# A fused RWKV and mixture-of-experts block: a reordered front, row differences on GpSimd, products of zeros at the start, one table for the slots' tokens

## The chip, the cores and the metric

The kernel runs on one core of a Trainium2 chip. The metric is the device time of one execution in microseconds. Three runs of the kernel before gave 666.15, 668.23 and 668.59 us, so the median is 668.23 us. Engines are named as in the profile: PE is the matrix engine, PEld its weight loads, DVE the vector engine, ACT the scalar engine, POOL is GpSimd, and SP issues most of the DMAs.

## The reference, cut to what matters

The input x has 2 x 2048 tokens of 256 channels. All weights are float32.

```
xn = layernorm(x)
# attention part (RWKV): a second layernorm with ln_g, ln_b
xa = layernorm(xn) * ln_g + ln_b
last = xa of the token before (zero for the first token of a sequence)
k, v, r = (xa*mix + last*(1-mix)) @ W.T          # one mix and one W for each of k, v, r
num, den = scans over the tokens: den = den*td + exp(k); num = num*td + exp(k)*v
attn = (sigmoid(r) * num/(den + 1e-8)) @ Wo.T
# expert part: 8 experts, the best 2 of each token
scores = relu(xn @ Wr + br);  weights = softmax over the best two
ffn = sum over the two: weight * (relu(xn @ W1[e] + b1[e]) @ W2[e] + b2[e])
out = x + attn + ffn
```

## The kernel before

The 4096 tokens are worked on in 8 blocks of 512 tokens (four groups of 128 partitions). The kernel has two parts. **The front** normalises, transposes and scores all blocks, chooses two experts for each token, sorts the 8192 (token, expert) pairs into slots of 128 rows that share one expert, and computes k, v and r. **The expert part** then walks over the slots: it gathers the slot's rows from a table in HBM, multiplies by W1 and W2 of the slot's expert (lines 818 and 831) and scatters the result with an add; the scans of the attention part (lines 697 to 729) run in between on DVE.

The order of the front is written out by hand: the schedule is manual, so every engine executes its instructions in the order of the program text, and each engine's queue is strictly in order. The pieces of the front, with the lines of the profile:

- `stats(b)` (187 to 196): DVE takes mean and variance of the block's four groups (8 instructions); POOL makes from them the factor `rr` by a power (193, 195) and a second value (196).
- `normed(b)` (214 to 222): DVE makes `mrr` from `rr`, then DVE normalises three groups (219) and ACT one (221); SP writes the rows to the table.
- `turned(b)` (232 to 240): POOL sets or copies the first column of `xaT` (the token before the block), PE transposes the rows (8 products, 238), ACT evacuates each half of the channels twice: `x2T` for the scores (239) and `xaT` for the attention (240).
- `scored(b)` and `routed(b)` (251 to 262): 8 small products for the scores, an evacuation by ACT, a transpose.
- `mix(n)`: the next n blends. A block has three (k, v, r). Ahead of a block's first one DVE makes the difference of neighbouring tokens `dx` (271, one buffer, 1024 elements a partition); a blend is two instructions on DVE (275).
- `some(n)`: the next n of 48 projection pieces, six for each block. A piece is two logical products (301, four records in the profile) and one evacuation by ACT (304). Blend number i, counted from 0, feeds pieces 2i and 2i+1.
- `divisors` (202): a power of 16 columns on POOL; `undivided` and `best_two` (206 to 353): the choice of experts on DVE, after all blocks are scored.
- then counts, ranks and positions of the pairs (484 to 576, mostly small DVE instructions), and the sorting into slots: eight rounds in which DVE builds tables `oh_a`, `oh_b` (645) and `oh_t` (656), and PE multiplies (665) for each of 8 columns `oh_a` by `oh_b` and by `oh_t` into the two halves of `inv`: the first half counts whether a slot's place is taken, the second holds its token number less 2048. DVE makes from both the rows to gather and to write (672 to 680); `experts_of_places` (590 to 632) finds the expert of each slot, `whose_i`.

The loads of the first slots' weights start once `whose_i` exists (the SP queue reads it into a register); the gathers start once `frm` (680) exists. Blends and pieces of the later blocks are spread among the steps after the choice of experts, so that PE has work beside them.

Of the kernel before, what the change touches and what calls it, by code (L numbers as in the profile page):

```python
# [9 lines left out]
F32 = mybir.dt.float32  # L10
# [16 lines left out]
def rwkv_moe_block(  # L27
# [21 lines left out]
    nc = tc.nc  # L49
# [130 lines left out]
    def stats(b):  # L180
        def mk(nm, shape):
            return rpool.tile(shape, F32, bufs=1, name=f"{nm}_{b}")

        st = mk("st", [P, NS, 6])
        mv = mk("mv", [P, NS, 2])
        for i in range(NS):
            nc.vector.bn_stats(st[:, i, :], xts[b][:, i, :])
            nc.vector.bn_aggr(mv[:, i, :], st[:, i, :])
        mean, var = mv[:, :, 0], mv[:, :, 1]

        at = ts(b, NS)
        w = mk("w", [P, NS])
# [4 lines left out]
        mrrs[b] = (mean, mk("mrr", [P, NS]))  # L197

    def divisors(half):

# [10 lines left out]
    def normed(b):  # L211
        xt = xts[b]
        mean, mrr = mrrs[b]
        nc.vector.scalar_tensor_tensor(mrr, mean, -1.0, rrs[b], ALU.mult, ALU.mult)
        x2 = x2s[b] = rpool.tile([P, NS, C], F32, tag="x2", bufs=3, name=f"x2_{b}")
        for t in range(NS):
            r, m = rrs[b][:, t : t + 1], mrr[:, t : t + 1]
            if t:
                nc.vector.tensor_scalar(x2[:, t, :], xt[:, t, :], r, m, ALU.mult, ALU.add)
            else:  # L220
                nc.scalar.activation(x2[:, t, :], xt[:, t, :], AF.Identity, bias=m, scale=r)
        nc.sync.dma_start(table_t[:, ts(b, NS), 0:C], x2)
# [3 lines left out]
    def turned(b):  # L226
        x2 = x2s[b]
        x2T = x2Ts[b] = rpool.tile([P, NC, TB], F32, tag="x2T", name=f"x2T_{b}")

        xaT = xaTs[b] = xa_pool.tile([P, NC, TB + 1], F32, name=f"xaT_{b}")  # L230
        if b % BPS == 0:
            nc.gpsimd.memset(xaT[:, :, 0:1], 0.0)
        else:
            nc.gpsimd.tensor_copy(xaT[:, :, 0:1], xaTs[b - 1][:, :, TB : TB + 1])
        for c in range(NC):
            tp = ps_t.tile([P, TB], F32, tag="pt", name=f"tp_{b}_{c}")
            for t in range(NS):
                nc.tensor.transpose(tp[:, ts(t, P)], x2[:, t, ts(c, P)], ident)
# [20 lines left out]
    def routed(b):  # L259
        i = b * NS % HT  # L260
        sp = sps[b * NS // HT][:, i : i + NS, :]
        nc.tensor.transpose(sp.rearrange("p t e -> p (t e)"), s8s[b], ident)

    blends = [[] for _ in range(NB)]

    def blender():
        for b in range(NB):
            now, last = xaTs[b][:, :, 1 : TB + 1], xaTs[b][:, :, 0:TB]

            dx = mixes.tile([P, NC, TB], F32, tag="dx", bufs=1, name=f"dx_{b}")  # L270
            nc.vector.tensor_tensor(dx, now, last, ALU.subtract)
            for i in range(3):
                m = mixes.tile([P, NC, TB], F32, tag="mix", name=f"mix{i}_{b}")
                for c in range(NC):
                    nc.vector.scalar_tensor_tensor(  # L275
                        m[:, c, :], dx[:, c, :], vec(1 + i, c), last[:, c, :],
                        ALU.mult, ALU.add,
                    )
                blends[b].append(m)
                yield  # L280
# [3 lines left out]
    def mix(n):  # L284
        for _ in range(n):
            next(blending)
# [115 lines left out]
    token = count("token", NT, F16, base=-NTOK // 2, step=P, chan=1)  # L402

    rest_row = rout.tile([P, NU], F32, name="rest_row")
    nc.gpsimd.iota(
# [9 lines left out]
    zero = rpool.tile([P, C], F32, bufs=1, name="zero")  # L415
    nc.gpsimd.memset(zero, 0.0)

    stats(2)
    normed(1)
    scored(0)  # L420
    turned(1)
    nc.scalar.activation(td, cols[:, E * NH : E * NH + NC], AF.Exp)
    mix(3)
    routed(0)
    scored(1)
    normed(2)
    some(2)
    turned(2)
    routed(1)
    stats(3)  # L430
    stats(4)
    normed(3)
    some(2)
    scored(2)
    turned(3)
    divisors(0)
    routed(2)
    mix(3)
    some(2)
    scored(3)  # L440
    routed(3)
    stats(5)
    normed(4)
    some(2)
    turned(4)
    stats(6)
    normed(5)
    some(1)
    scored(4)
    turned(5)  # L450
    stats(7)
    normed(6)
    routed(4)
    some(1)
    scored(5)
    turned(6)
    divisors(1)
    normed(7)
    routed(5)
    some(1)  # L460
    scored(6)
    turned(7)
    mix(3)
    routed(6)
    some(1)
    scored(7)
    routed(7)
    undivided()
    best_two()
    nc.sync.dma_start(  # L470
        b1cols.rearrange("e p h -> p e h"),
# [7 lines left out]
    some(4)  # L479


    pre = ps_t.tile([P, 2, E * NT], F32, tag="pt", name="pre")
# [10 lines left out]
    mix(3)  # L493
    some(2)
    cum = rt("cum", (P, E, NT))
    cum_flat = cum.rearrange("p e t -> p (e t)")
# [51 lines left out]
    nc.vector.tensor_tensor(pos, pos, be(delta), ALU.mult)  # L548
    nc.vector.tensor_tensor(pos, pos, rank, ALU.add)
    nc.vector.tensor_tensor(pos, pos, be(base_f), ALU.add)  # L550
    some(6)
    mix(3)
    some(6)
    mix(1)

    g2 = rt("g2", (P, NT))
    nc.gpsimd.tensor_tensor(g2, e2, g1, ALU.mult)
# [20 lines left out]
    mix(2)  # L578
    some(2)


# [53 lines left out]
        )  # L635


    inv = ps_y.tile([P, 2 * NU], F32, tag="py", name="inv")
    opool = routing.enter_context(tc.tile_pool(name="opool", bufs=3))
    for i0 in range(0, K * NT, CH):  # L640
# [21 lines left out]
        mix((0, 0, 0, 1, 0, 1, 0, 2)[i0 // CH])  # L662
        for i in range(CH):
            for j, right in enumerate((bq, bt_)):
                nc.tensor.matmul(
                    inv[:, j * NU : (j + 1) * NU], a[:, i // 2, :, i % 2],
                    right[:, i // 2, :, i % 2],
                    start=(i0 + i == 0 and j == 0), stop=(i0 + i == K * NT - 1 and j == 1),
                )
        some((1, 1, 1, 1, 1, 2, 1, 0)[i0 // CH])  # L670
    invs = rt("invs", (P, 2, NU))
    nc.vector.tensor_copy(invs, inv.rearrange("p (a u) -> p a u", a=2))
# [9 lines left out]
    experts_of_places()  # L682
    routing.close()
    gpool = ctx.enter_context(tc.tile_pool(name="gpool", bufs=3, side="right"))
    wpool = ctx.enter_context(tc.tile_pool(name="wpool", bufs=2, side="right"))
# [161 lines left out]
    load_first(0)  # L847
    load_second(0)
    load_first(1)
    some(6)  # L850
    unnorm(0)
    turn(0)
    some(2)
# [101 lines left out]
```

## Time and profile before

| what | value |
|---|---|
| median of three runs | 668.23 us |
| the profiled execution's own time | 668.74 us |
| its span, the stretch that the profile covers | 667.0 us |
| PE busy | 637.4 us (96%) |
| DVE busy | 342.7 us (51%) |
| ACT busy | 214.9 us (32%) |
| POOL busy | 237.5 us (36%) |
| first product of the expert part (line 818) starts at | 121.23 us |

The profile gives for each engine the busy time, and for each instruction its start, its length and, where the engine was idle before it, what ended the idle time. A group such as "x8" in a timeline is a row of equal instructions: its length runs from the start of the first to the end of the last, so the spacing of the instructions is a little less than the length divided by their number. Matmuls are pipelined; a single one is recorded with its latency, so spacings are what counts.

### The profile page before, as it was taken

The page shows a single profiled execution, that of the slowest core. Times are in us where ns is not written, and L with a number is a line of the kernel's source. Part 1 is how long each engine was busy: PE and PEld are TensorE (multiplying, and loading weights), DVE is VectorE, ACT ScalarE, POOL GpSimd, SP SyncE. Part 2 cuts the span into 40 slices and gives each one's busy share as a digit, 9 for nine tenths or more (in the row PEclk, how much of TensorE's full clock was granted, in tenths as well). Part 3 has the DMA queues.
Part 4 walks back from the last instruction along what each step waited for, and adds up shares of the span by engine and source line. Part 5 has one row for each costly group of instructions (what it writes and reads, how often), then busy time and mean ns, then how long its engine had stood idle before and what let it go on. Part 6 is the DMA issues. An engine that isn't in the chain of part 4 may idle for free. (4 is left out here: it accounts for less than half of the span.)

```text
span 667.0 us, 9213 instructions
## 1 busy us (share of the span) xinstructions
PE 637.4 (96%) x3109; PEld 501.6 (75%) x3109; DVE 342.7 (51%) x773; ACT 214.9 (32%) x452; POOL 237.5 (36%) x206
## 2 busy tenths in 40 slices
PE   3999999999999999999899999999999999999993
PEld 2454454688888888888688888888888888888882
DVE  7988998555545645646458675732222121222110
ACT  3683323332332342333233333232223222222320
POOL 5551203042342352350463543433434433434311
PEclk9999999999999999999999999999999999999997
DMA  8438101977887796798966877767566776566711
GB/s 283 162 129 268 16 1 42 333 213 221 231 237 231 202 275 196 198 304 274 305 141 163 259 176 210 176 194 197 171 176 182 212 221 210 169 175 188 214 27 17
DMA packets 94008, 126.73 MB, mean 190 GB/s; under 512 B 15644, under 2 KB 81896, under 8 KB 93832
## 3 DMA queue, kind: packets, MB, share of 16 engines
q1 hardware_dynamic: 75968, 103.22, 47.4%
q0 software_dynamic: 17472, 22.86, 18.3%
q8 instruction: 25, 0.41, 0.3%
q14 instruction: 23, 0.19, 0.1%
q10 hardware_dynamic: 520, 0.05, 0.1%
HBM read 108.12 MB, written 26.38 MB: 202 GB/s over the span
## 5 line engine op out<-in xcount | busy, mean ns | idle before, releaser
L818 PE MATMUL hp<-xT,w 128*128 128x256 f32 (+1 forms) x1216 | 254.1, 364 | 2.3 <-DMA w<-in_L_ffn_W_dram 1.2
L822 ACT ACTIVATE h<-hp,b 128x256 f32<-128x256 f32 (+1 forms) x304 | 138.2, 455 | 348.6 <-PE hp L818 256.4
L831 PE MATMUL yp<-w,h 128*128 128x256 f32 x1104 | 246.0, 381 | 0.0
L818 PEld LDWEIGHTS hp<-xT,w 128*128 128x128 f32 x1216 | 201.2, 189 | 51.0 <-ACT h L822 18.9
L831 PEld LDWEIGHTS yp<-w,h 128*128 128x128 f32 x1104 | 208.0, 191 | 27.0
L840 POOL DMA_INDIRECT out_dram<-y,into x48 | 80.4, 1675 | 192.3 <-DVE y L836 117.5
L808 DVE COPY xT<-xp 128x512 f32<-128x512 f32 (+1 forms) x38 | 24.4, 641 | 143.7 <-PE xp L806 143.7
L780 POOL DMA_INDIRECT xg<-table,frm x69 | 77.4, 1121 | 55.7 <-DVE mix L275 34.9
L835 DVE TENSOR_TENSOR y<-yp,b 128x256 f32<-128x256 f32 x69 | 29.2, 423 | 115.1 <-PE yp L831 114.5
L840 POOL DMA_INDIRECT acc<-y,into x21 | 33.7, 1603 | 99.6 <-DVE y L836 44.9
L720 DVE RECIPROCAL dn<-dn 128x512 f32<-128x512 f32 x16 | 53.7, 3353 | 0.5
L304 ACT ACTIVATE kvr<-p 128x512 f32<-128x512 f32 x48 | 28.6, 598 | 51.3 <-PE p L301 51.3
L791 DVE TENSOR_SCALAR xg<-xg 128x256 f32<-128x256 f32 x69 | 22.0, 353 | 31.6 <-DMA xg<-table,frm 31.6
L275 DVE SCALAR_TENSOR_TENSOR mix<-dx,cols,xaT 128x512 f32<-128x512 f32 x48 | 33.3, 756 | 0.4
L301 PE MATMUL p<-mix,wk 128*128 128x512 f32 x64 | 29.4, 599 | 0.1
L301 PE MATMUL p<-mix,wv 128*128 128x512 f32 x64 | 29.5, 596 | 0.0
L301 PE MATMUL p<-mix,wr 128*128 128x512 f32 x64 | 29.3, 596 | 0.0
L729 PE MATMUL op<-wo,z 128*128 128x256 f32 x128 | 28.9, 379 | 0.0
L836 DVE TENSOR_SCALAR y<-y,gate 128x256 f32<-128x256 f32 x69 | 25.7, 373 | 2.4
L729 PEld LDWEIGHTS op<-wo,z 128*128 128x128 f32 x128 | 24.3, 190 | 3.3
L806 PE MATMUL xp<-ident,xg 128*128 128x128 f32 x138 | 22.0, 276 | 3.0 <-DVE xg L791 3.0
L806 PEld LDWEIGHTS xp<-ident,xg 128*128 128x128 f32 x138 | 17.2, 142 | 7.1 <-DVE xg L791 3.5
(162 smaller groups left out, 363.5 us busy)
## 6 DMA issues: line engine op xcount, KB each, us to landing
w<-in_L_ffn_W_dram SPq DMA_DIRECT2D x76, 1024.0 KB, 7.8
b<-in_L_ffn_b_dram SPq DMA_DIRECT2D x38, 128.0 KB, 3.9
table<-x SPq DMA_DIRECT2D x8, 512.0 KB, 2.9
x<-in_L_attn_x_dram SPq DMA_DIRECT2D x7, 512.0 KB, 5.9
out_dram<-o_sb POOLq DMA_DIRECT2D x5, 512.0 KB, 5.8
acc<-o_sb POOLq DMA_DIRECT2D x3, 512.0 KB, 6.1
xg<-table,frm POOLq DMA_INDIRECT x69, 6.8
out_dram<-y,into POOLq DMA_INDIRECT x48, 7.5
```

The costliest lines, as they stand in the source:

```text
L275: nc.vector.scalar_tensor_tensor(m[:, c, :], dx[:, c, :], vec(1 + i, c), last[:, c, :], ALU.mult, ALU.add,)
L301: nc.tensor.matmul(p, w[:, c, ts(o, P)], m[:, c, :], start=(c == 0), stop=(c == NC - 1))
L304: nc.scalar.activation(kvr[b][:, i, o, :], p, f, scale=sign)
L720: nc.vector.reciprocal(dn, dn)
L729: nc.tensor.matmul(op, z[:, c, ts(t, P)], wo_sb[:, c, :], start=(c == 0), stop=(c == NC - 1))
L780: nc.gpsimd.indirect_dma_start(out=g, out_offset=None, in_=table, in_offset=bass.IndirectOffsetOnAxis(ap=frm[:, u : u + 1], axis=0), bound ...
L806: nc.tensor.transpose(xp[:, c, ts(i, P)], g[:, ts(c, P)], ident)
L818: nc.tensor.matmul(hp, w1_sb[:, c, ts(j, P)], xT[:, c, :], start=(c == 0), stop=(c == NC - 1))
L822: nc.scalar.activation(h[:, 0:n], hp, AF.Relu, bias=b1_sb[:, j : j + 1])
L831: nc.tensor.matmul(yp, hs[j][:, ts(i, P)], w2_sb[:, j, :], start=(j == 0), stop=(j == NH - 1))
L835: nc.vector.tensor_tensor(y, yp, b2_sb, ALU.add)
L840: return nc.gpsimd.indirect_dma_start(out=to, out_offset=bass.IndirectOffsetOnAxis(ap=into[:, u : u + 1], axis=0), in_=y, in_offset=None, ...
```

## The change

It has four parts.

1. **The order of the front.** `stats`, `normed`, `turned`, `scored`, `routed`, `mix` and `some` are called in another order, with mostly one piece at a time between the steps; for block 3 it reads `stats(3)`, `some(1)`, `scored(1)`, `mix(1)`, `normed(3)`, `some(1)`, `routed(1)`, `turned(3)`. Statistics of block 1 are split: two groups before `normed(0)`, two after it. For block 0 the two `xaT` evacuations come before the two `x2T` evacuations. Before the last score transpose (`routed(7)`) now stand 12 blends and 15 pieces (before: 9 and 12). Behind it come 5 pieces and the two products of line 484, with one blend beside them, then 2 pieces, the small DVE steps up to the positions (line 550), 2 pieces, two blends, 4 pieces, the pairs' places (568 to 576), one blend and 2 pieces. Two of the last four blends come after `experts_of_places` (before, all of the last came ahead of it). In the eight rounds of sorting stand one blend in every second round and 8 pieces (before: 4 blends and 8 pieces); after the first weight loads come 8 pieces, a transpose and 2 pieces (before: 6 and 2).
2. **The differences `dx`.** A function of its own, `differ(b)`, with two buffers. Block 0's is made on DVE in two halves, those of blocks 1 to 7 on POOL in one instruction each.
3. **Products of zeros.** 26 products of a zeroed bfloat16 tile, 512 columns wide, on PE: 20 first of all, 6 behind the transpose of the parameter rows. Nothing reads their result.
4. **One table.** The tokens of the second half of the columns are numbered one higher, so that no stored number is zero, and a place that is not taken holds exactly zero. The products with `oh_b` go (64 of 128), and the five DVE steps behind them are written anew: `inv == 0` says that the place is empty, `inv > 0` is taken off again.

The diff, cut to its core:

```
+        tps = []
         for c in range(NC):
             ...
-            nc.scalar.copy(x2T[:, c, :], tp)
+            tps.append(tp)
+            if b:
+                nc.scalar.copy(x2T[:, c, :], tp)
             nc.scalar.activation(
                 xaT[:, c, 1 : TB + 1], tp, AF.Identity, bias=vec(5, c), scale=vec(4, c)
             )
+        if b == 0:
+            for c in range(NC):
+                nc.scalar.copy(x2T[:, c, :], tps[c])
...
+    def differ(b):
+        now, last = xaTs[b][:, :, 1 : TB + 1], xaTs[b][:, :, 0:TB]
+        dx = dxs[b] = mixes.tile([P, NC, TB], F32, tag="dx", bufs=2, name=f"dx_{b}")
+        if b:
+            nc.gpsimd.tensor_tensor(dx, now, last, ALU.subtract)
+        else:
+            for c in range(NC):
+                nc.vector.tensor_tensor(dx[:, c, :], now[:, c, :], last[:, c, :], ALU.subtract)
...
-            dx = mixes.tile([P, NC, TB], F32, tag="dx", bufs=1, name=f"dx_{b}")
-            nc.vector.tensor_tensor(dx, now, last, ALU.subtract)
+            last, dx = xaTs[b][:, :, 0:TB], dxs[b]
...
+    idle = rpool.tile([P, TB], BF16, bufs=1, name="idle")
+    nc.vector.memset(idle, 0.0)
+    warm = ps_h.tile([P, TB], F32, tag="ph", name="warm")
+    def keep_warm(n):
+        for _ in range(n):
+            nc.tensor.matmul(warm, idle[:, 0:P], idle, start=True, stop=True)
+    keep_warm(20)
     stats(0)
...
-    stats(1)
+    keep_warm(6)
+    stats(1, 0, 2)
     normed(0)
+    stats(1, 2, NS)
     turned(0)
+    differ(0)
+    mix(1)
...
         for i in range(CH):
-            for j, right in enumerate((bq, bt_)):
-                nc.tensor.matmul(
-                    inv[:, j * NU : (j + 1) * NU], a[:, i // 2, :, i % 2],
...
+            nc.tensor.matmul(
+                inv, a[:, i // 2, :, i % 2], bt_[:, i // 2, :, i % 2],
+                start=(i0 + i == 0), stop=(i0 + i == K * NT - 1),
+            )
...
-    nc.vector.tensor_copy(invs, inv.rearrange("p (a u) -> p a u", a=2))
-    nc.vector.tensor_tensor(empty, invs[:, 0, :], less, ALU.mult)
-    nc.vector.tensor_tensor(row, invs[:, 1, :], empty, ALU.subtract)
-    nc.vector.tensor_tensor(into, row, rest_row, ALU.add)
+    nc.vector.scalar_tensor_tensor(empty, inv, 0.0, less, ALU.is_equal, ALU.mult)
+    nc.vector.tensor_scalar(row, inv, 0.0, None, ALU.is_gt)
+    nc.vector.tensor_tensor(row, inv, row, ALU.subtract)
+    nc.vector.scalar_tensor_tensor(into, row, float(NTOK // 2), empty, ALU.add, ALU.add)
...
     mix(2)
     experts_of_places()
+    mix(2)
...
-    some(6)
+    some(8)
     unnorm(0)
```

On POOL's queue the differences stand in this order: that of block 1 behind block 2's `rr`, that of block 2 behind block 4's, that of block 3 behind block 7's and ahead of the second `divisors`, that of block 4 behind it; that of block 5 ahead of the weights of the two experts (lines 557 to 563), those of blocks 6 and 7 behind them. The clearing of `xaT`'s first column for block 0 stands, as before, behind block 1's `rr` on POOL, and block 1's `rr` now waits for the two groups of statistics that come after `normed(0)`.

More of the change, by code (lines that the diff above doesn't have):

```diff
@@ L178, in rwkv_moe_block, with mk, stats @@
     rrs, mrrs, xaTs = [None] * NB, [None] * NB, [None] * NB
[L180 to L186, printed above, removed]
+    sts, mvs = [None] * NB, [None] * NB
+    def mk(nm, shape):
+        return rpool.tile(shape, F32, bufs=1, name=nm)
+    def stats(b, i0=0, i1=NS):
+        if i0 == 0:
+            sts[b], mvs[b] = mk(f"st_{b}", [P, NS, 6]), mk(f"mv_{b}", [P, NS, 2])
+        st, mv = sts[b], mvs[b]
+        for i in range(i0, i1):
             nc.vector.bn_stats(st[:, i, :], xts[b][:, i, :])
             nc.vector.bn_aggr(mv[:, i, :], st[:, i, :])
+        if i1 < NS:
+            return
         mean, var = mv[:, :, 0], mv[:, :, 1]
         at = ts(b, NS)
-        w = mk("w", [P, NS])
+        w = mk(f"w_{b}", [P, NS])
         nc.gpsimd.tensor_scalar(w, var, 1.0 + LN_EPS, LN_EPS * LN_EPS, ALU.mult, ALU.add)
@@ L196, in stats @@
         nc.gpsimd.tensor_scalar(ve_all[:, at], var, LN_EPS, 0.0, ALU.add, ALU.add)
-        mrrs[b] = (mean, mk("mrr", [P, NS]))
+        mrrs[b] = (mean, mk(f"mrr_{b}", [P, NS]))
     def divisors(half):
@@ L264, in rwkv_moe_block @@
     blends = [[] for _ in range(NB)]
+    dxs = [None] * NB
+    def differ(b):
[6 more added lines that the diff above has]
+                nc.vector.tensor_tensor(dx[:, c, :], now[:, c, :], last[:, c, :], ALU.subtract)
     def blender():
         for b in range(NB):
-            now, last = xaTs[b][:, :, 1 : TB + 1], xaTs[b][:, :, 0:TB]
-            dx = mixes.tile([P, NC, TB], F32, tag="dx", bufs=1, name=f"dx_{b}")
-            nc.vector.tensor_tensor(dx, now, last, ALU.subtract)
+            last, dx = xaTs[b][:, :, 0:TB], dxs[b]
             for i in range(3):
@@ L401, in rwkv_moe_block @@
     u_iota = count("u_iota", NSING, base=2 * NPAIR * P, step=P)
-    token = count("token", NT, F16, base=-NTOK // 2, step=P, chan=1)
+    token = rout.tile([P, NT], F16, name="token")
+    for i in range(2):
+        nc.gpsimd.iota(
+            token[:, i * HT : (i + 1) * HT], [[P, HT]], base=(-NTOK // 2, 1)[i],
+            channel_multiplier=1, allow_small_or_imprecise_dtypes=True,
+        )
     rest_row = rout.tile([P, NU], F32, name="rest_row")
@@ L416, in rwkv_moe_block @@
     nc.gpsimd.memset(zero, 0.0)
-    stats(2)
     normed(1)
-    scored(0)
+    some(1)
     turned(1)
     nc.scalar.activation(td, cols[:, E * NH : E * NH + NC], AF.Exp)
-    mix(3)
+    mix(1)
+    some(1)
+    stats(2)
+    scored(0)
+    differ(1)
+    mix(1)
+    normed(2)
+    some(1)
     routed(0)
+    turned(2)
+    stats(3)
+    some(1)
     scored(1)
-    normed(2)
-    some(2)
-    turned(2)
+    mix(1)
+    normed(3)
+    some(1)
     routed(1)
-    stats(3)
+    turned(3)
     stats(4)
-    normed(3)
-    some(2)
+    differ(2)
+    some(1)
     scored(2)
-    turned(3)
+    mix(1)
+    normed(4)
+    some(1)
+    routed(2)
+    turned(4)
+    stats(5)
     divisors(0)
-    routed(2)
-    mix(3)
-    some(2)
+    some(1)
     scored(3)
[L441 to L446, printed above, removed]
+    mix(1)
     normed(5)
     some(1)
+    routed(3)
+    turned(5)
+    stats(6)
+    some(1)
     scored(4)
-    turned(5)
+    normed(6)
+    some(1)
+    routed(4)
+    turned(6)
     stats(7)
-    normed(6)
-    routed(4)
+    differ(3)
+    divisors(1)
     some(1)
     scored(5)
-    turned(6)
-    divisors(1)
+    mix(2)
     normed(7)
+    some(1)
     routed(5)
-    some(1)
+    turned(7)
     scored(6)
-    turned(7)
-    mix(3)
-    routed(6)
+    mix(1)
     some(1)
     scored(7)
+    routed(6)
+    mix(3)
+    some(1)
     routed(7)
     undivided()
+    differ(4)
     best_two()
@@ L478, in rwkv_moe_block @@
     kvr_late = ctx.enter_context(tc.tile_pool(name="kvr_late", bufs=NB // 2, side="right"))
-    some(4)
+    some(5)
     pre = ps_t.tile([P, 2, E * NT], F32, tag="pt", name="pre")
@@ L492, in rwkv_moe_block @@
     nc.gpsimd.tensor_scalar(tot, e2, 1.0, 0.0, ALU.add, ALU.add)
-    mix(3)
+    mix(1)
     some(2)
@@ L550, in rwkv_moe_block @@
     nc.vector.tensor_tensor(pos, pos, be(base_f), ALU.add)
-    some(6)
-    mix(3)
-    some(6)
-    mix(1)
+    some(2)
+    mix(2)
+    some(4)
+    differ(5)
     g2 = rt("g2", (P, NT))
@@ L577, in rwkv_moe_block @@
     lo, hi = lohi[:, 0, :], lohi[:, 1, :]
-    mix(2)
+    differ(6)
+    mix(1)
     some(2)
@@ L635, in experts_of_places @@
         )
-    inv = ps_y.tile([P, 2 * NU], F32, tag="py", name="inv")
+    inv = ps_y.tile([P, NU], F32, tag="py", name="inv")
     opool = routing.enter_context(tc.tile_pool(name="opool", bufs=3))
+    MIX, SOME = (0, 1, 0, 1, 0, 1, 0, 1), (1, 1, 1, 2, 1, 1, 1, 0)
     for i0 in range(0, K * NT, CH):
@@ L661, in rwkv_moe_block @@
         )
-        mix((0, 0, 0, 1, 0, 1, 0, 2)[i0 // CH])
+        mix(MIX[i0 // CH])
         for i in range(CH):
-            for j, right in enumerate((bq, bt_)):
-                nc.tensor.matmul(
-                    inv[:, j * NU : (j + 1) * NU], a[:, i // 2, :, i % 2],
[L667 to L672, printed above, removed]
+            nc.tensor.matmul(
+                inv, a[:, i // 2, :, i % 2], bt_[:, i // 2, :, i % 2],
+                start=(i0 + i == 0), stop=(i0 + i == K * NT - 1),
+            )
+        some(SOME[i0 // CH])
+    differ(7)
     empty = rt("empty", (P, NU))
-    nc.vector.tensor_tensor(empty, invs[:, 0, :], less, ALU.mult)
+    nc.vector.scalar_tensor_tensor(empty, inv, 0.0, less, ALU.is_equal, ALU.mult)
     row = rt("row", (P, NU))
-    nc.vector.tensor_tensor(row, invs[:, 1, :], empty, ALU.subtract)
+    nc.vector.tensor_scalar(row, inv, 0.0, None, ALU.is_gt)
+    nc.vector.tensor_tensor(row, inv, row, ALU.subtract)
     into = const.tile([P, NU], I32, name="into")
-    nc.vector.tensor_tensor(into, row, rest_row, ALU.add)
+    nc.vector.scalar_tensor_tensor(into, row, float(NTOK // 2), empty, ALU.add, ALU.add)
     frm = const.tile([P, NU], I32, name="frm")
@@ L682, in rwkv_moe_block @@
     experts_of_places()
+    mix(2)
     routing.close()
@@ L849, in rwkv_moe_block @@
     load_first(1)
-    some(6)
+    some(8)
     unnorm(0)
```

## The prediction

> **What bounds the kernel now.** I read the busy table by stretches first (columns: PE, PEld, DVE, ACT, POOL busy with the instructions, the clock granted to PE, DMA share, GB/s).
>
> ```profile
> 10.00:20.00 10.00, 8.92 (x55) 5.32 (x56) 9.75 (x24) 6.23 (x13) 9.15 (x20) 1.00 1.06 343
> ...
> 30.00:40.00 10.00, 9.23 (x60) 4.50 (x59) 9.32 (x34) 6.27 (x13) 4.16 (x9) 1.00 0.16 54
> ...
> 51.20:80.00 28.80, 28.03 (x67) 12.15 (x67) 27.40 (x61) 9.08 (x16) 5.52 (x7) 1.00 0.44 128
> 80.00:121.20 41.20, 40.07 (x213) 19.78 (x211) 35.53 (x86) 12.55 (x21) 5.67 (x5) 1.00 0.18 46
> 121.20:667.00 545.80, 530.69 (x2582) 448.50 (x2582) 236.43 (x493) 160.19 (x352) 197.15 (x141) 0.99 0.71 202
> ```
>
> The expert part is PE's: 530.7 of 545.8 us, and the change leaves it as it is. So the question is when its first product starts, now 121.23 us. In the front PE and DVE are both nearly full. Next, the waits of the front (waiter, releaser, us in all, times, longest) show how tightly the two are coupled:
>
> ```profile
> DVE score L339 <- PE sp L262: 1.9, 1, 1.9
> DVE invs L672 <- PE inv L665: 1.6, 1, 1.6
> PE hp L818 <- DMA w<-in_L_ffn_W_dram: 1.2, 1, 1.2
> PE pre L484 <- DVE hot L353: 0.6, 1, 0.6
> ```
>
> Third, PE's timeline gives the prices (start, length, count):
>
> ```profile
> 9.94 1.97 PE L238 MATMUL tp<-ident,x 128*128 128x128 f32 x8 [2.02 <-ACT x L221]
> ...
> 17.58 0.83 PE L301 MATMUL p<-mix,wk 128*128 128x512 f32 x1
> ...
> 43.34 1.09 PE L238 MATMUL tp<-ident,x 128*128 128x128 f32 x8 [0.22 <-ACT x L221]
> 44.27 0.27 PE L262 MATMUL sp<-ident,s 128*128 128x128 f32 x1
> 44.38 1.88 PE L301 MATMUL p<-mix,wr 128*128 128x512 f32 x4
> 46.19 0.64 PE L251 MATMUL p<-x2T,wr_sb 128*32 128x128 f32 x16
> ```
>
> By the starts, a block's transposes cost 0.93, the score transpose 0.11, a lone piece 1.81, a block's scores 0.64. Pieces in a row cost 1.717 (eight records in 3.43). PE's first piece starts only at 17.58: until there it waits, and its transposes take 1.97 instead of 1.09.
>
> **The change, step by step**
>
> *Start to first piece.* Block 1's first two statistics (0.53 each from 6.97) end at 8.03, `mrr` follows at 8.1 (`rr` is ready at 7.93, as now), the three normalisations (0.97) end at 9.2, the other two statistics at 10.25. Block 0's difference needs the cleared column of `xaT`, which POOL writes behind block 1's `rr`. Today that stretch runs from 9.28 to 10.95, or 1.67; from 10.35 it ends at 12.0. The two halves of the difference (1.21 today in one) end at 13.3, the first half blend (0.75) at 14.1. First piece at 14.1 instead of 17.58: **3.5 us earlier**. The moved column, not the statistics, sets this.
>
> *Zeros.* They must not reach past that cover. They start near 2.2, after DVE's memsets. A bfloat16 product of 256 columns at line 484 takes 0.105 by its start to the next, so one of 512 takes 0.21 on a PE at speed; the first transposes go at 0.24 apiece against 0.11 later, so a slow one may take 0.45. All 26: 5.5 to 11.7. I take slow for the first eight: 20 end near 8.3, `colp` and six more near 10.0, the transposes' halves at 10.5 and 11.0, the `xaT` evacuations (0.8, starting 0.67 apart) near 12.1: just covered. Without the zeros, blocks 0 and 1 would pay 0.9 each in slow transposes, mostly under the same cover, so I count no gain. The granted clock reads 1.00 in all these stretches, so it doesn't show this slowness; the row lengths do. [...]
>
> *To the end of the last score transpose.* PE has 15 lone pieces (27.2), 7 blocks' transposes (6.5), 8 scores (5.1), 8 score transposes (0.9): 39.7, so 53.8 without waits. Today's stretch, 17.58 to 51.16, holds 31.5 of the same kinds (four pairs of pieces, four lone) and 2.1 of waits. A block of the new order asks 5.3 of PE and 4.65 of DVE (2.13 statistics, 1.19 normalising, 1.33 blend), so PE leads by a little; I take 0.8 of waits: **54.6**, with three pieces more behind it than today (51.16 and 12).
>
> *The differences.* DVE loses seven of 1.26. What POOL pays isn't shown for this size. The nearest rows are 256 elements:
>
> ```profile
> 66.25 0.63 POOL L559 TENSOR_TENSOR r<-hot,g 128x256 f32<-128x256 f32 x1
> 69.92 0.80 POOL L560 TENSOR_TENSOR r<-hot,g 128x256 f32<-128x256 f32 x1 [3.04 <-DVE pos L549]
> 70.80 1.58 POOL L562 TENSOR_TENSOR rw<-r,r 128x256 f32<-128x256 f32 x1
> ```
>
> Four times that is 2.5 to 6.3 us each. I take 3: line 562 writes with a stride, the difference does not. In return DVE slows beside POOL:
>
> ```profile
> 43.21 1.22 DVE L271 TENSOR_TENSOR dx<-xaT 128x1024 f32<-128x1024 f32 x1
> 44.47 4.07 DVE L275 SCALAR_TENSOR_TENSOR mix<-dx,cols,xaT 128x512 f32<-128x512 f32 x6
> ...
> 70.15 1.65 DVE L271 TENSOR_TENSOR dx<-xaT 128x1024 f32<-128x1024 f32 x1
> 71.83 4.55 DVE L275 SCALAR_TENSOR_TENSOR mix<-dx,cols,xaT 128x512 f32<-128x512 f32 x6
> ```
>
> Beside 3.27 us of POOL's lines 560 to 563 the same work took 0.91 longer; beside POOL's power (43 to 47) nothing. So each difference takes back 0 to 0.9 of DVE's 1.26. [...]
>
> *Is DVE late?* From 13.3: 12 blends (16.0), 7 normalisings (8.3), 6 statistics (12.8), the divisors and first score (0.95), the choice (7.05): 58.4. Block 6's `rr` stands behind the power of 16 columns (3.4) and comes 2.2 late: 60.6. Four differences take 0 to 3.6: 60.6 to 64.2. PE wants `hot` after five pieces, at 54.6 + 8.7 = 63.3. So PE waits 0 to 0.9; today 0.65.
>
> *To the first product.* Behind the last score transpose PE has 33 pieces (56.7), line 484's pair (0.2), the sorting, the first slot's transposes (0.6). One sorting round of 16 products takes 0.63 with its switch; 0.0355 a product, so eight fewer leave 0.35: 2.8 in all instead of 5.1. Switches 0.4, waits taken 0.6: 61.3. **54.6 + 61.3 = 115.9.** Today: 36 pieces and 121.23.
>
> *Cover checks.* `inv` is ready at 54.6 + 8.7 + 17.2 (ten pieces) + 0.6 + 16.6 (eight rounds with eight pieces) + 0.2 = 97.9. DVE's five steps (1.3), two blends (2.7) and the experts (4.3) give `whose_i` at 106.2. Today's 7.15 from there to the product (114.08 to 121.23) makes 113.4: the weights come 2.5 ahead. If DVE slips more than that, it's the weights' wait that is late next. The last blends fall at about 108 and 109.3, the pieces that read them at 107.5 and 111: tight. The gathers move up with `frm` (99 instead of 107), SP's queue holds nothing new.
>
> **Sum.** 121.23 - 115.9 = 5.3 us off the span of 667.0; the expert part is carried over unchanged. The profiled run took 668.74, the median is 668.23: I set 668.2 - 5.3 = **662.9 us**.
>
> **Rivals**
>
> 1. *No waits* and pieces at 1.72 where I took 1.81: 0.8 + 0.6 + 1.4 less, **660.1**. For it: the 1.09 row shows only 0.22 of wait a block. Against: DVE and PE are within 1 us at several places. 0.12.
> 2. *DVE stays the late one*: every difference takes its full 0.9, `hot` 0.9 late, then again 1.1 at the first sorting table, and a normalising late by 0.9 where three differences stand: 2.0 + 2.7 - 1.4 allowed, **666.2**. For it: lines 271 and 275 at 70 us. Against: statistics, not blends, stand beside two of the differences. 0.12.
> 3. *Zeros stay slow*: 26 at 0.45 end near 14.3, evacuations at 15.6 instead of 12.1: 3.5 late, **666.4**. 0.06.
> 4. *Slower: POOL's queue.* A difference at 6.3 (line 562's rate) stands ahead of block 3's `rr`, block 5's, and the second power that the scores need. Block 3's `rr` has 2.9 for the difference (POOL free at 21.0, wanted with its 1.6 at 25.5). Each of the three places then loses up to 3.4: about 9 with the overlap, **671.9**. PE stands still with the normalising. It decides from 2.9; at about 4.7 a difference the gain is gone (3 x 1.8 = 5.4). For it: POOL and DVE slow each other in the rows above. Against: 0.63 and 0.80. 0.10.
>
> The forecast, 661 to 665, holds 0.60. The range reaches from 658.5, below rival 1, to 668.5, past rivals 2 and 3, and leaves out rival 4 and a little at each end. Within 0.5% (3.3 us) is about what a measurement can tell from no change. Faster by more: the forecast, rival 1 and a sliver of 2, 0.73. Within: the rest of 2 and 3 and the low side of 4, 0.19. Slower: 0.08.
>
> **What would show it.** First piece near 14.1, with DVE waiting for POOL's cleared column; zeros ending near 10; the differences at 2.5 to 3.5; the last score transpose near 54.6; `hot` within 1 us of PE's wish; the first line-818 product near 116 without a wait for its weights; the rest 545 to 546 long. Wrong, if a difference passes 4.7, if `mrr` waits for POOL by over 3 us a block, or if the expert part changes length.

## The result, and the profile after

The changed kernel took 677.97 us (median of four runs, 676.4 to 678.38) against 668.41 us for the kernel before (four runs, 666.15 to 670.76). The ratio is 1.014, with an interval of 1.0115 to 1.0164. The forecast was 662.9: it is **slower by 9.6 us where 5.3 less was expected**. In the profiled execution the span is 676.6 us (before 667.0).

The changed kernel's busy table, in stretches like those shown of before (columns: PE, PEld, DVE, ACT, POOL busy with the instructions, granted clock, DMA share, GB/s; the cuts are the last score transpose, the first sorting round and the first product of the expert part):

```profile
10.00:20.00 10.00, 7.35 (x28) 3.82 (x25) 7.95 (x21) 5.24 (x11) 7.28 (x19) 0.83 1.07 347
30.00:40.00 10.00, 8.58 (x48) 4.36 (x46) 8.71 (x24) 6.54 (x13) 4.15 (x5) 1.00 0.24 86
62.20:90.30 28.10, 26.35 (x64) 11.50 (x63) 26.93 (x64) 9.67 (x17) 10.06 (x10) 1.00 0.46 131
90.30:131.30 41.00, 37.46 (x140) 17.32 (x140) 30.30 (x73) 10.15 (x17) 7.86 (x6) 0.92 0.28 85
131.30:676.60 545.30, 530.49 (x2583) 449.38 (x2581) 237.05 (x493) 160.41 (x353) 197.56 (x141) 0.99 0.70 200
```

The last row is the expert part: 545.3 us, as before (545.8). All of the loss lies in front of it: its first product starts at 131.35 instead of 121.23. In the front PE is less full than before in every row (8.58 of 10 instead of 9.23 from 30 to 40), and in two rows the granted clock is below 1.00 (0.83 and 0.92), which it was in no row of the front before.

PE's timeline, after, with the places to look at:

```profile
9.20 1.46 PE L383 MATMUL warm<-idle 128*128 128x512 bf16 x6
10.49 1.04 PE L244 MATMUL tp<-ident,x 128*128 128x128 f32 x8
14.18 3.67 PE L320 MATMUL p<-mix,wk 128*128 128x512 f32 x4 [2.65 <-DVE mix L294]
...
62.14 0.27 PE L273 MATMUL sp<-ident,s 128*128 128x128 f32 x1
...
121.39 0.41 PE L862 MATMUL xp<-ident,xg 128*128 128x128 f32 x2 [0.34 <-DVE xg L847]
124.98 0.69 PE L862 MATMUL xp<-ident,xg 128*128 128x128 f32 x2 [3.19 <-DVE xg L847]
125.46 6.05 PE L320 MATMUL p<-mix,wr 128*128 128x512 f32 x8
```

The first piece starts at 14.18, as forecast (14.1), but takes 3.67 where a lone piece takes 1.88 (work that is slow behind idle time is called cold below). The last score transpose stands at 62.14, where 54.6 was forecast. And at the end PE waits for the rows of the first slot (3.19), after which two pieces take 6.05 instead of 3.60. So there are two holes: **7.5 us between the first piece and the last score transpose**, and **some 6 us at the rows of the first slot**. What lies between them took about what was forecast (62.7 from the last score transpose to the first product once the gather is mended, in e1_place below, against 61.3).

The waits of the front, PE's and DVE's (waiter, releaser, us in all, times, longest):

```profile
PE xp L862 <- DVE xg L847: 3.5, 2, 3.2
PE p L320 <- DVE mix L294: 2.7, 1, 2.7
PE tp L244 <- DVE x L224: 2.6, 3, 1.1
PE warm L383 <- DVE restart L172: 2.2, 1, 2.2
PE p L320 <- ACT kvr L323: 2.0, 6, 0.4
PE inv L721 <- DVE oh_t L713: 1.5, 1, 1.5
```

```profile
DVE mrr L219 <- POOL rr_all L200: 5.1, 5, 1.4
```

Two of these are new or grown: pieces that wait for ACT (six times, never before), and `mrr` on DVE that waits for the power on POOL (0.3 in all before).

Where does the first hole come from? POOL's and DVE's timelines in the same microseconds show one cause. POOL first, with a difference and the first gather; then DVE:

```profile
22.36 1.89 POOL L282 TENSOR_TENSOR dx<-xaT 128x1024 f32<-128x1024 f32 x1
...
117.28 1.51 POOL L836 DMA_INDIRECT xg<-table,frm  x1 [17.66 <-DVE mix L294]
```

```profile
22.29 2.11 DVE L224 TENSOR_SCALAR x<-x,rr_all,mrr 128x256 f32<-128x256 f32 x1
```

A difference takes POOL 1.89 us, less than the 3 assumed. But the normalising instruction that starts beside it takes 2.11 us instead of 0.4: it ends about when the difference ends (24.40 and 24.25). VectorE is held up by GpSimd's instruction; below this is called the hold-up. And the gather, on POOL's queue behind nothing, starts at 117.28 although `frm`, the list that it reads, is written at 108.29.

### The profile page after: what moved, and what is told of

It is laid out like the page before. It is cut to its first block, busy times and chain, and to the rows that moved or that the text cites. A ratio compares the mean times of both kernels' runs of the same rounds, so it can differ in the third digit from the quotient of the medians.

```text
span 676.6 us, 9153 instructions
## 1 busy us (share of the span) xinstructions
PE 647.0 (96%) x3071; PEld 503.6 (74%) x3071; DVE 344.3 (51%) x768; ACT 214.8 (32%) x452; POOL 253.7 (37%) x214
## 5 line engine op out<-in xcount | busy, mean ns | idle before, releaser
L864 DVE COPY xT<-xp 128x512 f32<-128x512 f32 (+1 forms) x38 | 24.3, 640 | 138.8 <-PE xp L862 138.8
L320 PE MATMUL p<-mix,wk 128*128 128x512 f32 x64 | 32.0, 632 | 3.3 <-DVE mix L294 2.7
L320 PE MATMUL p<-mix,wr 128*128 128x512 f32 x64 | 32.0, 639 | 0.6 <-ACT kvr L323 0.6
```

The lines of the kernel that those rows point to most:

```text
L320: nc.tensor.matmul(p, w[:, c, ts(o, P)], m[:, c, :], start=(c == 0), stop=(c == NC - 1))
```

## The experiments

Each kernel was run beside the kernel before (whose medians were 666.55 to 668.02); the ratios are to those runs. Theory: (1) the second `dx` buffer moves memory so that the gather waits for a later instruction; (2) a difference on POOL holds VectorE up for about as long as it saves; (3) the order has waits and a cold start that the forecast didn't count. Rival: the new order itself cannot be faster, because VectorE bounds the front however it is arranged.

### The gather: memory, not data

In the changed kernel the gather (117.28) starts 1.0 after the end of the DVE instruction at line 688, the last of `experts_of_places`, which comes two blends and some twenty small instructions after `frm`:

```profile
115.80 0.48 DVE L688 TENSOR_TENSOR mine<-whose,e_iota 128x320 f32<-128x320 f32 x1
```

Nothing there is read by the gather. But the buffer that it writes belongs to a new pool (`gpool`), opened when the pool of the routing's tiles is closed, and the second `dx` buffer takes 4 KB more of each partition. If that pushes the routing's pool into the memory of `gpool`, the gather has to wait for the last instruction that used this memory, whatever it reads. The addresses aren't in the profile; the next two runs test the reading.

**e1_place**: the changed kernel, with two tiles put into the memory of dead ones:

```
-    rank = rt("rank", (P, E, NT))
+    rank = rt("rank", (P, E, NT), tag="prio")
...
-    pos = rt("pos", (P, E, NT))
+    pos = rt("pos", (P, E, NT), tag="cand")
...
-    r1, r2 = rt("r1", tag="cum"), rt("r2", tag="rank")
+    r1, r2 = rt("r1", tag="cum"), rt("r2", tag="prio")
```

> The changed kernel, with two routing tiles sharing the memory of dead ones, so that the routing pool is 2 KB a partition smaller and ends where the pool of the gathered rows begins; nothing else differs. Theory (the second difference buffer of 4 KB pushed the routing pool under the rows' pool, so the first gather waits for the last routing instruction, line 688): the first gather starts near 109.3 instead of 117.28, PE does not wait 3.2 for the rows nor slow down behind it, the first product of line 874 comes near 125.4 instead of 131.35, span 670 to 671, time about 672. Rival (the two blends moved behind the experts' step delay the gathers): nothing changes, 676 to 678.

Measured: 672.42 us, ratio 1.0074 (1.0049 to 1.0098), span 670.8. POOL's gather and PE's timeline:

```profile
109.72 1.60 POOL L836 DMA_INDIRECT xg<-table,frm  x1 [9.78 <-DVE mix L294]
```

```profile
121.19 0.60 PE L862 MATMUL xp<-ident,xg 128*128 128x128 f32 x4
121.63 3.60 PE L320 MATMUL p<-mix,wr 128*128 128x512 f32 x8
125.07 7.24 PE L874 MATMUL hp<-xT,w 128*128 128x256 f32 x32
```

The gather follows `frm`, PE waits for no rows, the pieces take 3.60 again, and the first product is 6.3 us earlier. The second hole is closed; no instruction was taken out for it, only the memory of two tiles was changed.

**e2_before_buf2**: the kernel before, with nothing but the second buffer:

```
-            dx = mixes.tile([P, NC, TB], F32, tag="dx", bufs=1, name=f"dx_{b}")
+            dx = mixes.tile([P, NC, TB], F32, tag="dx", bufs=2, name=f"dx_{b}")
```

> The kernel before, with two buffers for the difference instead of one and nothing else. Theory of the pushed pool: the first gather waits for line 632 (ends at 114.99 before) and starts near 116 instead of 108.11; PE waits about 4 for its rows and goes on at a lower clock; first product near 126, span 671 to 673. Rival (the order is the cause, a buffer is harmless): span 666 to 667.5.

Measured: 678.07 us, ratio 1.0142 (1.0102 to 1.0182), span 676.3. One buffer more, which nothing needs, costs as much as the whole change. The first gather before, and then in this run, where the profile names line 632 (688 of the changed kernel) as what it waited for:

```profile
108.11 1.60 POOL L780 DMA_INDIRECT xg<-table,frm  x1 [34.92 <-DVE mix L275]
```

```profile
116.84 1.32 POOL L780 DMA_INDIRECT xg<-table,frm  x1 [42.81 <-DVE mine L632]
```

PE's timeline of this run, and its busy table from 120 to 130:

```profile
124.33 0.66 PE L806 MATMUL xp<-ident,xg 128*128 128x128 f32 x2 [7.29 <-DVE xg L791]
126.02 0.69 PE L806 MATMUL xp<-ident,xg 128*128 128x128 f32 x2 [1.03 <-DVE xg L791]
126.50 5.17 PE L301 MATMUL p<-mix,wr 128*128 128x512 f32 x8
```

```profile
120.00:130.00 10.00, 4.64 (x9) 2.31 (x10) 2.37 (x10) 0.01 (x1) 2.85 (x3) 0.52 0.98 336
```

The mechanism was as expected (gather at 116.84 instead of 108.11), the price twice as high. Two things come on top of the late start. The loads of the weights are issued from 116.60 on, just ahead of the gather; the DMA engines are 98% busy from 120 to 130, and VectorE gets the first rows at 123.88, 7.0 after the gather's start (a gather before landed 3.1 after its issue, in the median of five). And in the stretch that holds most of the 7.29 us of idling, and the pieces behind it, PE is granted 0.52 of its clock.

### The differences

**e3_dx_dve**: e1_place with all differences on DVE, at the same places of the order.

```
         if b:
-            nc.gpsimd.tensor_tensor(dx, now, last, ALU.subtract)
+            nc.vector.tensor_tensor(dx, now, last, ALU.subtract)
```

> The changed kernel with the smaller routing pool (span 670.8, first product of the expert part at 125.07), and the seven differences of blocks 1 to 7 taken by VectorE again, at the same places of the order. Hold-up theory (a difference on GpSimd holds one VectorE instruction for 1.3 to 1.7, about 10 us in all): VectorE takes 7 x 1.26 = 8.8 us more of its own and loses the 10 us of hold-ups, and the powers on GpSimd no longer stand behind a difference: about even, span 668.5 to 671, the three normalising instructions of 2.5 to 2.8 us back at 1.1, and the waits of mrr for rr shorter than 5.1 in all. The forecast's step (on GpSimd they cost VectorE 0 to 0.9 in all): VectorE's work grows by 8 us, 4 to 6 of them ahead of `hot`: span 674 to 677.

Measured: 669.59 us, ratio 1.0032 (1.0013 to 1.0050), span 667.5, first product 2.6 us earlier than in e1_place. DVE's groups to 120 us (busy us, mean ns), first of the changed kernel and then of e3_dx_dve:

```profile
L224 DVE TENSOR_SCALAR x<-x,rr_all,mrr 128x256 f32<-128x256 f32 x24 | 13.7, 624 | 0.9 <-DVE mrr L219 0.6
...
L702 DVE TENSOR_TENSOR oh_b<-hi_iota,lohi 128x568 f16<-128x568 f16 x8 | 5.3, 659 | 0.0
...
L623 DVE TENSOR_TENSOR at<-pos,hot 128x256 f32<-128x256 f32 x2 | 2.3, 1155 | 0.0
L212 DVE TENSOR_TENSOR sd<-rs,inv_rr 128x32 f32<-128x32 f32 x1 | 1.6, 1573 | 0.1
L556 DVE CAST ni<-cum 128x8 int32<-128x8 f32 x1 | 1.4, 1446 | 0.0
```

```profile
L224 DVE TENSOR_SCALAR x<-x,rr_all,mrr 128x256 f32<-128x256 f32 x24 | 8.9, 429 | 0.8 <-DVE mrr L219 0.2 <-PE sp L273 0.2
L282 DVE TENSOR_TENSOR dx<-xaT 128x1024 f32<-128x1024 f32 x7 | 8.5, 1211 | 1.1 <-ACT td L460 1.1
...
L702 DVE TENSOR_TENSOR oh_b<-hi_iota,lohi 128x568 f16<-128x568 f16 x8 | 3.6, 448 | 0.0
...
L623 DVE TENSOR_TENSOR at<-pos,hot 128x256 f32<-128x256 f32 x2 | 1.2, 594 | 0.0
...
L212 DVE TENSOR_TENSOR sd<-rs,inv_rr 128x32 f32<-128x32 f32 x1 | 0.2, 192 | 0.1
...
L556 DVE CAST ni<-cum 128x8 int32<-128x8 f32 x1 | 0.2, 171 | 0.0
```

In these five groups DVE is busy for 24.3 us with the differences on POOL and 14.1 without: 10.2 us go into the hold-up of seven instructions, 1.46 for each difference. The differences themselves cost DVE 8.5. So moving them saved nothing, and among the instructions that are held are the three normalisings that PE's transposes wait for. Not everything is held: beside the difference at 83.68 a `TENSOR_REDUCE` of 256 elements (line 624) took 0.42, as it does in e3_dx_dve.

**e5_no_dx**: e1_place without any difference for blocks 1 to 7; the blends read the rows in its place, so the output is not the block's.

```
+        if b:
+            return
...
-        if b:
-            nc.gpsimd.tensor_tensor(dx, now, last, ALU.subtract)
-        else:
+        if b == 0:
...
-            last, dx = xaTs[b][:, :, 0:TB], dxs[b]
+            last, dx = xaTs[b][:, :, 0:TB], dxs[b] if b == 0 else xaTs[b][:, :, 1 : TB + 1]
```

> The changed kernel with the smaller routing pool, and no differences for blocks 1 to 7: the blends read the rows themselves in the place of the difference, so the differences of seven blocks are left out and the output is not the reference's. Hold-up theory: the 10 us of hold-ups go and nothing is put in their place; some 5 to 6 us of them lie ahead of `hot` (now at 71.2), the others in the sorting: first product at 117 to 121 instead of 125.07, span 663 to 667. The forecast's step (a difference on GpSimd costs VectorE next to nothing): no more than 1 us earlier, span 669.8 to 670.8.

Measured: 665.19 us, ratio 0.9966 (0.9951 to 0.9981), span 665.3, first product at 119.41 instead of 125.07. So the seven differences cost 5.7 us on GpSimd, where the forecast had them as a gain.

**e4_before_dx_pool**: the kernel before with all eight differences on POOL and one buffer.

```
-            nc.vector.tensor_tensor(dx, now, last, ALU.subtract)
+            nc.gpsimd.tensor_tensor(dx, now, last, ALU.subtract)
```

> The kernel before, with the eight differences on POOL at their places in the program (one buffer). Theory (a difference on POOL takes 1.9 and holds up one DVE instruction for most of that, 1.1 to 1.7, as in the changed kernel, and block 0's stands on the path to the first piece): DVE gains nothing, span 667 to 672. Rival (the forecast's: POOL relieves DVE by 1.26 each and gives back at most 0.9): span 661 to 666.

Measured: 680.45 us, ratio 1.0194 (1.0160 to 1.0228), span 677.9. Slower than either theory had it. Its wait at DVE says why: in this order the blends stand right behind their difference, so DVE waits for POOL besides being held.

```profile
DVE mix L275 <- POOL dx L271: 19.9, 5, 5.5
```

### The other parts

**e6_one_table**: the kernel before with only the one-table sum (part 4 of the change).

```
-                nc.tensor.matmul(
-                    inv[:, j * NU : (j + 1) * NU], a[:, i // 2, :, i % 2],
...
+            nc.tensor.matmul(
+                inv, a[:, i // 2, :, i % 2], bt_[:, i // 2, :, i % 2],
...
```

> The kernel before, with the one-table sum alone. Theory: 64 products of 0.0355 less on an engine that is the bound in the sorting, 2.3 off the span: 664.4 to 665.2. Rival (DVE's tables set the pace of the rounds, so the products' end stays): 666.5 to 667.5.

Measured: 665.50 us, ratio 0.9981 (0.9963 to 1.0000), span 663.3. The interval ends at 1, so the time alone hardly shows a gain. In the profile the first product moves from 121.23 to 119.14, and it waits longer for its weights (1.54 instead of 1.16):

```profile
119.14 3.14 PE L820 MATMUL hp<-xT,w 128*128 128x256 f32 x13 [1.54 <-DMA w<-in_L_ffn_W_dram]
```

**e7_zeros**: the kernel before with only the products of zeros.

```
+    keep_warm(20)
     stats(0)
...
+    keep_warm(6)
     stats(1)
```

> The kernel before with the products of zeros alone: 20 at the start, 6 behind colp. The first block's transposes take 1.04 instead of 1.97, as in the changed kernel, but the first piece waits for VectorE's blends (17.58) both ways, and TensorE idles for 2 us or more ahead of it: theory: nothing gained or lost, span 666.4 to 667.4. Rival (the zeros carry the full clock over to the first pieces): 1.5 to 2.5 us less, span 664.5 to 665.5. Second rival (the zeros delay colp and with it the first scales): 0.5 to 1 us more.

Measured: 668.12 us, ratio 1.0008 (0.9993 to 1.0024); first product at 120.76. No difference that this measurement can show.

**e8_warm**: e3_dx_dve with zeros in the hole ahead of the first blend.

```
     turned(0)
+    keep_warm(12)
     differ(0)
```

> The kernel with the differences on VectorE and the smaller routing pool, and 12 more products of zeros behind the first block's transposes, which fill the 2.65 us in which TensorE waits for the first blend. Both theories: the first piece takes about 1.8 instead of 3.5 us. If TensorE bounds the first part from there on (the forecast's reading: one piece and one block after another), all later work moves up by 1.7: span 1.7 less than the same kernel without them. If VectorE bounds it (what the waits of the transposes for x now say), the pieces only wait longer for x: 0 to 0.5 less.

Measured: 668.28 us, ratio 1.0016 (0.9998 to 1.0034), span 666.7, last score transpose at 59.06 instead of 60.15, first product at 121.26 instead of 122.49. PE's timeline, with the first piece and the third block's transposes:

```profile
13.87 1.98 PE L320 MATMUL p<-mix,wk 128*128 128x512 f32 x4
...
23.12 1.23 PE L244 MATMUL tp<-ident,x 128*128 128x128 f32 x8 [1.46 <-ACT x L226]
```

The piece is 1.7 faster, of which 1.2 reach the end; a part turns into a wait for `x`. Between the two expectations, so both engines bind in turns.

**e9_p8**: e8_warm with the scores in another pool of PSUM, where this kernel's products go.

```
-        p8 = ps_a.tile([P, P], F32, tag="pa", name=f"p8_{b}")
+        p8 = ps_h.tile([P, P], F32, tag="ph", name=f"p8_{b}")
```

> The kernel with the differences on VectorE, the smaller routing pool and the 12 products behind the first transposes (span 666.7, last score transpose at 59.06, first product of the expert part at 121.26), with the score products in a PSUM buffer of their own pool, so that the pieces have their two buffers to themselves. Theory (a piece behind the scores waits 0.32 to 0.41 for ScalarE to empty the buffer of the piece before, six times, 2.0 in all, because the scores take the other buffer): these waits go; the waits of the transposes for x (2.0) grow by a part of it, since VectorE is not faster: last score transpose 0.8 to 2.0 earlier, span 665 to 666.5. Rival (VectorE bounds everything up to the choice of experts): last score transpose no more than 0.3 earlier, span unchanged.

Measured: 667.31 us, ratio 1.0003 (0.9985 to 1.0022), span 663.6. The six waits for ACT (2.0) are gone from the list, but the last score transpose moved only 0.45, to 58.61, about as much as a start can vary between runs. PE waits longer for `x` (2.4 instead of 2.0) and 0.7 for a blend, and the piece at 23.85, behind a wait of 1.80, took 3.52, where in e8_warm it took 1.88 behind 1.46. Between the two expectations again, nearer to the rival. The span fell by more than the front did, in the expert part, which none of this touches; the front's times are the ones to read.

**e10_stats**: e9_p8, with DVE's idle stretches filled by statistics taken ahead.

```
     stats(1, 2, NS)
+    stats(2, 0, 3)
     turned(0)
...
+    stats(4, 0, 2)
     normed(3)
...
+    stats(6, 0, 2)
     normed(5)
...
+    stats(7, 0, 2)
     normed(6)
```

The later calls take the groups that are left, as in `stats(4, 2, NS)`.

> The kernel with the scores in their own PSUM buffer, and parts of the statistics of blocks 2, 4, 6 and 7 taken earlier (three groups of block 2 into VectorE's idle 1.9 us near 10, two groups of blocks 4, 6 and 7 ahead of the normalising of the block before), so that mrr does not wait for the power on GpSimd. Theory (VectorE's waits for rr, 3.8 in all, and its idle start are what the order lost to the forecast): those waits fall below 1.5, x comes 1.5 to 3 earlier, last score transpose at 54.5 to 56.5 (forecast 54.6, now 59.06), hot 2.5 to 3.5 earlier, first product at 117 to 119, span 662.5 to 664.5. Rival (TensorE does not gain, as the sorting and the last blends are VectorE's and lie behind): first product at 120 to 121, span 665.5 to 666.5.

Measured: 664.87 us, ratio 0.9945 (0.9924 to 0.9967), span 662.5: **faster than both kernels**. PE's timeline, and its waits to 135 us apart from the start:

```profile
56.20 0.27 PE L273 MATMUL sp<-ident,s 128*128 128x128 f32 x1
...
118.58 7.24 PE L879 MATMUL hp<-xT,w 128*128 128x256 f32 x32
```

```profile
PE inv L726 <- DVE oh_t L718: 1.3, 1, 1.3
PE tp L244 <- ACT x L226: 1.2, 1, 1.2
```

The rival falls: the last score transpose comes 2.4 earlier, at 56.20. Of this 1.64 is the piece that took 3.52 in e9_p8: here it takes 1.88, behind a wait of 1.17. The two waits are 2.5 us. The forecast had allowed 1.4 for waits, so they explain some 1.1 of the 2.7 by which 118.58 misses its 115.9.

**e11_experts**: e6_one_table, with the experts of the slots between the last two blends.

```
-    mix(2)
+    mix(1)
     experts_of_places()
+    mix(1)
```

> The kernel before with the one-table sum, and the experts of the slots found between the last two blends instead of behind both. Theory (its first product, at 119.14, waits 1.54 for the weights, whose loads start behind the experts): the loads start 1.4 earlier, the last blend is still ahead of its pieces: first product at 117.7 to 118, span 661.7 to 662.3. Rival (the weights' loads are bound by the DMA engines, not by their start): first product at 119, no change.

Measured: 664.70 us, ratio 0.9958 (0.9941 to 0.9976), but its first product came no earlier: at 120.16, and 68.7 us behind its last score transpose, where e6_one_table took 68.4. The theory is wrong. `whose_i` is written 0.7 us earlier, and still SP issues the first load only here:

```profile
113.76 0.36 SPq L766 DMA_DIRECT2D b<-b1cols  x1
```

That is right behind the last blend (112.15 to 113.47), and SP's own wait in the profile names it:

```profile
SPq L766 <- DVE mix L275: 1.5, 1, 1.5
```

The load reads nothing of a blend. That it waits for the memory of the closed pool, like the gather, is argued and not tested by itself. So finding the experts earlier brings no load forward while a blend stands behind it, and the lower median isn't explained by this edit.

**e12_pool_again**: e10_stats with the seven differences back on POOL.

```
-            nc.vector.tensor_tensor(dx, now, last, ALU.subtract)
+            nc.gpsimd.tensor_tensor(dx, now, last, ALU.subtract)
```

> The fastest version so far (span 662.5, last score transpose at 56.20, first product of the expert part at 118.58), with the seven differences back on GpSimd and nothing else changed. Hold-up theory: each difference follows rr on GpSimd's queue and so starts when the normalising starts on VectorE, and holds one of its instructions for about 1.7; x comes that much later for three blocks, and one instruction is held at each of the four other places: last score transpose 2 to 4 later, first product at 120.5 to 122.5, span 664.5 to 667. The forecast's step (0 to 0.9 of the 1.26 given back): VectorE has 2.5 to 8.8 less to do, the waits that are left on TensorE (2.5) shrink: first product at 116.5 to 118.6, span 660.5 to 662.5.

Measured: 667.60 us, ratio 0.9990 (0.9974 to 1.0006), span 666.4; last score transpose at 58.18, first product at 120.89, 2.0 and 2.3 later than in e10_stats. These are the hold-up theory's numbers, the first at its lower edge, in an order where PE had waits to give away. The differences of blocks 1 to 3 stand beside a normalising again (2.48 to 2.76 for three instructions); that of block 4 now stands beside blends, where in the changed kernel it held a step of 32 elements. DVE's timelines, e10_stats and then e12_pool_again:

```profile
50.41 5.39 DVE L294 SCALAR_TENSOR_TENSOR mix<-dx,cols,xaT 128x512 f32<-128x512 f32 x8
```

```profile
52.41 7.01 DVE L294 SCALAR_TENSOR_TENSOR mix<-dx,cols,xaT 128x512 f32<-128x512 f32 x8
```

Blends are held as well, by 1.62.

## Why the prediction was wrong

From the changed kernel to e10_stats each step mends one thing, and the first product of the expert part moves with it:

| kernel | mended | last score transpose | first product |
|---|---|---|---|
| changed | | 62.14 | 131.35 |
| e1_place | the gather's wait | 62.42 | 125.07 |
| e3_dx_dve | the differences | 60.15 | 122.49 |
| e8_warm | the cold first piece | 59.06 | 121.26 |
| e9_p8 | the scores' PSUM buffer | 58.61 | 120.71 |
| e10_stats | DVE's idle time | 56.20 | 118.58 |
| forecast | | 54.6 | 115.9 |

Each row is one profiled execution. Their first pieces start between 13.81 and 14.45, so a step of a few tenths, such as that of e9_p8, isn't told apart from such a shift.

- **"The gathers move up with `frm` (99 instead of 107)": wrong, and the largest step, 6.3 us.** The check asked when the data are ready, and not when the memory is free. The diff shows the second buffer; the prediction passed over it.
- **"Each difference takes back 0 to 0.9 of DVE's 1.26": wrong**, 2.6 us. The duration on POOL was overestimated (1.89, 3 taken), but DVE's loss is 1.46 for each difference, more than its own 1.21. The 0.91 in the profile of before was the loss beside four instructions that overlapped only in part; in the changed kernel each of the seven held instructions ends 0.03 to 0.38 behind the end of its difference. Why it falls on the normalising: the difference stands behind `rr` on POOL's queue, and the normalising starts when `rr` is there, so the two meet in three blocks of three. Rival 2 had the mechanism, priced at 0.9 each.
- **"I take 0.8 of waits" from the first piece to the last score transpose: wrong**, by 7.5 us, of which 2.3 is the hold-up. The runs name the others: the cold first piece (1.1 at that place), perhaps the PSUM buffer (0.45), and DVE's idle time, most of it `mrr` waiting for the power (2.4, with 1.64 of e9_p8's slow piece in it). The prediction added up DVE's work in a block (4.65) against PE's (5.3) and took the difference for slack; but the statistics, the power on POOL and the normalising are a chain, and with one blend or none between them DVE stands still at the power. Some 1.6 remain. In e10_stats PE waits 1.2 for `x` (0.8 were allowed), and four blocks' transposes take 1.07 to 1.33 from their start to the next instruction instead of the 0.93 of the sum, 0.9 in all.
- **`hot` at 60.6 to 64.2: wrong** (71.2), for the same reasons; 65.0 in e10_stats.
- **The first piece at 14.1: right** (14.18), and DVE did wait for the cleared column (1.8). **The zeros' end near 10.0: right within 0.5** (10.5), but they were slow for longer than taken: the first twelve are about 0.43 apart, and 20 took 7.10 where 6.1 was added up. The eight were the author's estimate, and no run shows them. And the prediction did not ask what the idle time after them costs: behind 2.65 us of it the first piece was cold (3.67). By themselves the zeros bring nothing that e7_zeros can show.
- **One table, 5.1 to 2.8: right** (2.3 less): 2.1 in e6_one_table, with PE waiting 0.4 longer for weights.
- **61.3 from the last score transpose to the first product: right but for the gather**, 62.4 in e10_stats and 62.7 in e1_place (69.2 in the changed kernel).
- **The weights 2.5 ahead: right that PE doesn't wait, wrong in the reason.** The loads follow the blends that were put behind `experts_of_places`, and not `whose_i`: in e10_stats `whose_i` is written at 108.68 and the first load issued at 112.61. From there to the first product it is 5.97, against 6.04 before, where PE did wait for the weights. The reserve is gone.
- **The expert part unchanged: right** (545.3 against 545.8).
- **Rival 4, POOL's queue: wrong in kind.** Its condition, a difference longer than 2.9 us on POOL (4.7 for the gain to be gone), wasn't met, and no wait of `mrr` passes 1.4. The kernel is slower for a reason that no rival named.

With the place, the differences, the cold piece, the PSUM buffer and the idle time mended, nearly the same order gives 664.87 us, 3.2 less than the kernel before beside it (668.02). The forecast's 5.3 less comes nearer to that kernel than to the one in the diff. What stays open is the cause of the last 1.6 us of the order, which no run separated, and why e11_experts has a lower median than e6_one_table without an earlier first product (the two intervals overlap).

## What to carry to other kernels

When a change adds a buffer, ask what memory it pushes, and read for each DMA of the next stage which instruction it waits for; a released pool is a wait like any other (8.7 us for the first gather in e2_before_buf2). Before work goes from VectorE to GpSimd, look at what VectorE does at that very moment: count most of the length of the moved instruction as lost on VectorE (here 1.46 of 1.89 to 2.27) and move it only beside work that is shown to go on. And where two engines are nearly full, sum up the chain through a block and not only each engine's work.

## What the runs showed of the hardware

- The hold-up works both ways, and mostly what started first goes on: five of the seven instructions that were held in the changed kernel start 0.2 to 0.8 behind their difference, the other two within 0.1 of it. On POOL a four-element step takes 0.19 alone (e8_warm, at 9.96); beside DVE's difference it takes 1.09 and beside blends 0.60, here in e8_warm, where DVE makes the differences:

```profile
19.63 1.09 POOL L198 TENSOR_SCALAR w<-mv 128x4 f32<-128x4 f32 x1 [2.04 <-DVE mv L191]
...
54.63 3.96 POOL L239 COPY xaT<-xaT 128x2 f32<-128x2 f32 x1
```

  The second is a copy of two elements that waits through a row of eight blends (53.16 to 58.54) and ends at 58.59. Held on DVE in the changed kernel were a TENSOR_SCALAR of 0.4, which took 2.11 beside a difference of 1.89, a CAST of 0.17, which took 1.45, and a TENSOR_TENSOR of 32 elements, which took 1.57 instead of 0.19. A TENSOR_REDUCE with one input went on (0.42). Whether statistics go on beside a difference no run shows.
- PE's work can be slow behind idle time, and not always at once. In the changed kernel the piece behind 2.65 us without work took 3.67, with a granted clock of 0.83 from 10 to 20, and in e5_no_dx the one behind 3.40 took 3.75; with zeros in the hole the first piece took 1.98 (e8_warm). In e1_place the piece behind 3.51 us of idling took 1.98, and a later one, behind waits of 0.98 and 1.19, took 3.27, with a granted clock of 0.83 from 20 to 30. In e9_p8 a piece behind a wait of 1.80 took 3.52, in e8_warm the same piece behind 1.46 took 1.88. So the length of a wait alone doesn't tell which work will be slow, and no run shows what decides it.
- GpSimd subtracts 1024 float32 elements a partition in 1.89 us in most rows, and in 2.64 at the most (e4_before_dx_pool, beside VectorE's tables). Four times the rows with 256 elements would have given 2.5 to 6.3, so the short rows say little about the long one.
